# Two graph layers on one core: the order of the first loads, and which engine does the set-up of the tables and batch norms

## The chip, the core and the metric

The kernel runs on 1 core of one Trainium2 chip, in one launch, with all arithmetic in float32. The metric is the device time in microseconds (us): the median of 3 runs before the change is 1963.95 us (1963.61 to 1965.49).

The engines are called as the profile calls them: PE is TensorE (matmul), PEld its weight load, DVE is VectorE, ACT is ScalarE, POOL is GpSimd, SP is SyncE. SPq, ACTq and so on are their instruction queues, from which DMAs are issued too.

## The reference

For each of 128 batches of 128 nodes with D = 256 features, layer 0 is a residual graph convolution, and layer 1 a convolution block, a distance-weighted message pass and a GRU. Cut to what the change touches:

```python
# layer 0, per batch:  x [128, 256], adj [128, 128]
norm  = (adj.sum(-1) + 1e-6) ** -0.5
f_hom = adj @ ((x @ theta) * norm) * norm
f_het = x @ W_h
gate  = sigmoid(x @ W_t + b_t)
x     = layernorm(x + elu(gate * f_hom + (1 - gate) * f_het))
# layer 1: 1x1 convolution, batch norm 1, relu, convolution of 17 taps along the nodes, batch norm 2
h = relu(bn1(conv1d(x.T, conv1_w)))
x_conv = relu(bn2(conv1d(h, conv2_w, pad=8)) + x.T)
# ... messages A @ relu(x @ w_msg + b_msg) with A = exp(-dist), then a GRU cell, then a layernorm
```

`bn(h) = h * scale + (b - m * scale)` with `scale = g / sqrt(v + 1e-5)`: four vectors of 256 each for both norms. The kernel does the 17-tap convolution through a cosine and sine transform of length L = 136, so it needs a table of cosines and sines (`T`, and `A` for the nodes), which it computes on the chip.

## The kernel before

**Three stages.** Stage A does layer 0 and the 1x1 convolution for 64 pairs of batches (J = 2), and turns the 17-tap weights into their transform on the side. Stage B multiplies in the transformed domain. Stage C does the rest of layer 1. The change lies in the set-up and in the first rounds of stage A.

**The rounds of stage A.** `a_round(t)` runs for t = -1 to 63 under a schedule written out by hand: on each engine, instructions stand in the order of the code, and an engine's queue is strictly in order. Round t does the projections of pair t (`l0_project`: `f_ps`, `gate_ps` on PE; `hom`, `het` from ACT), in the middle of which `between()` puts the gate of pair t-1, and behind which `beside()` puts the turn of the next x (`l0_turn`, DVE transposes of `xb` to `xT`), the ELU and statistics of pair t-1 (`l0_elu`) and the degrees of the next adjacency (`l0_degrees`: two PE transposes, a DVE reduce, and `inv_sqrt`, two small POOL instructions). Then follow the layer norm of pair t-1 (`l0_norm`; its `rstd` too comes from `inv_sqrt` on POOL), the 1x1 convolution of pair t-3, the DMA issues on SP, and `l0_mix` of pair t. From pair 4 on the turn of the next x stands at the end of the round, and the next round's `f_ps` waits for it. `xT` has one buffer apart from that of pair 1, so the turn of pair 3 waits until PE has read pair 2's.

**The set-up that is woven in** is written as generators, and each `next(...)` emits one part at its place:

- `tables` (`table`, L211 on) computes the table on tiles of 128x272: range reduction on DVE, then a polynomial of degree 8 in `w` (L239 to L242), then three small instructions that make sums and differences of cosine and sine (L248 to L250). All of it is on DVE; it has one `yield`, so the first part stands in round -1 ahead of the turn of pair 0, the second behind the degrees of pair 0.
- `norms` (`batch_norms`): part 1 turns the first norm's vectors on PE (`vec_ps`, L260), copies them on DVE (`col`, L261) and takes `inv_sqrt` on POOL; part 2 is three small DVE instructions and four ACT `diag`; part 3 is a PE broadcast (`row_ps`) from which DVE makes `shift1` (L276) and scales `conv1_w` (L278). The parts stand in rounds 0, 1 and 2.
- `ways` (`way_back`): part 1 spreads a piece of `A` into `AL` on DVE (L283) and clears tiles on POOL; part 2 turns both on PE and makes `S` and `SL` on DVE (L294, L295).

**The first loads.** SP issues the four parts of the first pair's x (`xb`), then `adjT` of pair 0, then `W_t`, then x and adjacency of pair 1. ACT issues `theta`, `W_h`, `b_t`, a table load and a tanh, and eight small loads for the norms (`vec`, `col`). The part ahead of the rounds is ordered by the framework's scheduler. The compiled program gives its DMAs eight completion semaphores in turn, so that each DMA waits at its issue for the eighth before it to have landed.

## Time and profile before

| | |
|---|---|
| median of 3 runs (lowest, highest) | 1963.95 us (1963.61, 1965.49) |
| the profiled execution: device time | 1964.43 us |
| its span, from first to last instruction | 1962.6 us |
| what lies around the span | 1.8 us |
| PE, DVE, ACT, POOL busy, share of the span | 99%, 77%, 38%, 34% |
| granted PE clock, mean | 0.998 |
| first real matmuls start (adjacency of pair 0; first `f_ps`) | 8.95 us; 9.19 us |
| first `f_ps` of pairs 1, 2, 3, 4 | 16.13, 22.37, 32.41, 42.16 us |

Times in the views are from the start of the span. The timeline gives start, duration, engine, line, operation, output <- inputs, shapes, the number of merged instructions, and in brackets how long the engine had been idle before and what ended that. The chain of waits gives start, length and what the end of the kernel hung on at that moment.

### The profile page before, as it was taken

To read this page: it belongs to the slowest core of one execution; us is meant where nothing else is said; L and a number is where in the kernel's file an instruction comes from. 1 tells how busy PE (TensorE), PEld (TensorE's weight loads), DVE (VectorE), ACT (ScalarE), POOL (GpSimd) and SP (SyncE) were. 2 spreads that over 40 slices of the span, in tenths; PEclk is the share of its full clock that TensorE was granted. 3 is DMA by queue.
4 is the path that set the end of the run, shared out by engine and by line. 5 is a ranking of instruction groups with operands and counts; after the bars stand their busy time and mean duration, and the time that the engine had idled before them with its cause. 6 is when DMAs were issued, how large, how long until landed. Compare 5 with 4: busy or idle time off the path is not lost.

```text
span 1962.6 us, 26741 instructions
## 1 busy us (share of the span) xinstructions
PE 1938.2 (99%) x8539; PEld 1323.9 (67%) x8539; DVE 1502.2 (77%) x3031; ACT 738.7 (38%) x1493; POOL 670.6 (34%) x887
## 2 busy tenths in 40 slices
PE   8999999999999999999999999999999999999997
PEld 5666666666666888866666666666666666666664
DVE  8888888888888644477777777877778777787776
ACT  4666666666666311122223322222222232223222
POOL 2111111111111355544344434434433452543431
PEclk9999999999999999999999999999999999999999
DMA  6787777877776899952212212221221222121100
GB/s 175 209 239 220 232 213 232 244 226 221 224 230 188 282 324 334 321 184 93 71 59 72 82 60 65 72 71 60 82 80 45 72 82 70 61 77 38 43 28 22
DMA packets 334660, 279.90 MB, mean 143 GB/s; under 512 B 150735, under 2 KB 276921, under 8 KB 334521
## 3 DMA queue, kind: packets, MB, share of 16 engines
q1 hardware_dynamic: 327817, 272.68, 45.1%
q10 hardware_dynamic: 6704, 5.52, 0.9%
q8 instruction: 69, 1.13, 0.2%
q14 instruction: 70, 0.57, 0.1%
HBM read 173.26 MB, written 104.86 MB: 142 GB/s over the span
## 4 chain that ended last, share of the span: by engine, by line
PE 94%; DVE 3%; DMA 1%; ACT 1%; issue 1%; POOL 1%; SPq 0%; ACTq 0%; POOLq 0%; DVEq 0%
PE g_ps L1123 43%; PE f_ps L357 11%; PE y_ps L806 6%; PE gate_ps L362 5%; PE conv_ps L449 5%; PE msg_ps L977 4%; PE coef_ps L470 3%; PE z_ps L819 3%; PE conv_ps L923 3%; PE nmp_ps L1055 3%; PE mix_ps L383 3%; PE w_ps L486 2%; PE wl_ps L513 1%; PE conv_ps L930 1%; PE adj_ps L337 1%
## 5 line engine op out<-in xcount | busy, mean ns | idle before, releaser
L318 ACT ACTIVATE y<-y,nb_b,rstd_b 128x256 f32<-128x256 f32 x128 | 70.0, 593 | 562.3 <-DVE nb_b L316 562.3
L357 PE MATMUL f_ps<-w,xT 128*128 128x512 f32 x512 | 244.6, 600 | 3.0 <-DVE xT L427 1.8
L1166 POOL TENSOR_TENSOR u<-u,p 128x512 f32<-128x512 f32 x63 | 79.9, 1268 | 249.5 <-DVE p L1146 240.9
L357 PEld LDWEIGHTS f_ps<-w,xT 128*128 128x128 f32 x512 | 89.1, 189 | 103.4 <-issue 67.1
L1123 PE MATMUL g_ps<-t_h,sh 128*128 128x384 f32 x384 | 156.8, 490 | 0.0
L1123 PE MATMUL g_ps<-t_c,sc 128*128 128x384 f32 x384 | 155.2, 486 | 0.0
L1123 PE MATMUL g_ps<-t_m,sm 128*128 128x384 f32 x384 | 155.2, 486 | 0.0
L362 PEld LDWEIGHTS gate_ps<-w,xT 128*128 128x128 f32 x512 | 97.2, 190 | 68.3 <-issue 53.6
L192 POOL TENSOR_SCALAR rstd_a<-mv_a 128x2 f32<-128x2 f32 x64 | 12.2, 191 | 362.2 <-DVE mv_a L309 257.6
L362 PE MATMUL gate_ps<-w,xT 128*128 128x256 f32 x512 | 131.5, 379 | 0.1
L806 PE MATMUL y_ps<-wb,H 128*128 128x256 f32 x544 | 128.4, 379 | 0.0
L814 POOL TENSOR_TENSOR ws<-wb 128x512 f32<-128x512 f32 x67 | 93.9, 1404 | 88.3 <-PE z_ps L819 52.0
L449 PE MATMUL conv_ps<-conv_w,x1T 128*128 128x259 f32 x512 | 122.6, 381 | 1.0 <-DVE x1T L427 1.0
L366 ACT ACTIVATE hom<-f_ps,norm 128x256 f32<-128x256 f32 x128 | 60.7, 474 | 141.8 <-PE f_ps L357 133.5
L806 PEld LDWEIGHTS y_ps<-wb,H 128*128 128x128 f32 x544 | 103.4, 190 | 14.0
L1082 ACT ACTIVATE o<-o 128x1024 f32<-128x1024 f32 (+1 forms) x65 | 67.6, 1040 | 113.6 <-POOL o L1167 58.7
L449 PEld LDWEIGHTS conv_ps<-conv_w,x1T 128*128 128x128 f32 x512 | 97.1, 190 | 16.4 <-PE w_ps L486 1.8
L1123 PEld LDWEIGHTS g_ps<-t_c,sc 128*128 128x128 f32 x384 | 73.0, 190 | 50.9
L1123 PEld LDWEIGHTS g_ps<-t_m,sm 128*128 128x128 f32 x384 | 73.0, 190 | 50.9 <-DVE sm L1071 0.2
L1123 PE MATMUL g_ps<-w_hhT_w,cx1T 128*128 128x384 f32 x256 | 105.1, 492 | 0.0
L1123 PE MATMUL g_ps<-w_ihT_w,nmpT 128*128 128x384 f32 x256 | 103.8, 487 | 1.2 <-ACT nmpT L1059 1.2
L1123 PE MATMUL g_ps<-w_ihT_w,xcT 128*128 128x384 f32 x256 | 103.6, 486 | 1.2 <-ACT xcT L944 1.2
(243 smaller groups left out, 4400.9 us busy)
## 6 DMA issues: line engine op xcount, KB each, us to landing
wb<-w_d SPq DMA_DIRECT2D x68, 512.0 KB
w_d<-w_o SPq DMA_DIRECT2D x32, 1024.0 KB
y_d<-yb SPq DMA_DIRECT2D x68, 256.0 KB
x<-in_x SPq DMA_DIRECT2D x64, 256.0 KB
x_d<-x SPq DMA_DIRECT2D x64, 256.0 KB
cx1T<-x1T_d SPq DMA_DIRECT2D x64, 256.0 KB
yt<-y_d SPq DMA_DIRECT2D x32, 512.0 KB
cx<-x_d SPq DMA_DIRECT2D x32, 512.0 KB
```

The costliest lines, as they stand in the source:

```text
L318: nc.scalar.activation(dst[:, q, :], src[:, q, :], AF.Identity, bias=nb[:, q : q + 1], scale=rstd[:, q : q + 1],)
L357: nc.tensor.matmul(pf, lhsT=xT[:, c, nodes(j)], rhs=w0[:, c, 0 : 2 * D], start=(c == 0), stop=(c == NC - 1),)
L362: nc.tensor.matmul(pg[:, j * D : (j + 1) * D], lhsT=xT[:, c, nodes(j)], rhs=w0[:, c, 2 * D : 3 * D], start=(c == 0), stop=(c == NC - 1),)
L366: nc.scalar.activation(hom[:, j, :], pf[:, 0:D], AF.Copy, scale=norm[:, j : j + 1])
L383: nc.tensor.matmul(pm[:, j * D : (j + 1) * D], lhsT=adjT_[:, j, :], rhs=hom[:, j, :], start=True, stop=True,)
L449: nc.tensor.matmul(ph[:, 0 : D + CO], lhsT=s["x1T"][:, c, nodes(j)], rhs=conv1_w[:, c, :], start=(c == 0), stop=(c == NC - 1),)
L806: nc.tensor.matmul(py[:, blk, :], lhsT=coefs(blk if k == 0 else 2 * k + 1 - blk, c), rhs=w[:, blk, c, :], start=(c == 0), stop=(c == NC - 1),)
L814: nc.gpsimd.tensor_tensor(ws, w[:, 0], w[:, 1], ALU.add)
L977: nc.tensor.matmul(pm[:, pr * P : (pr + 1) * P], lhsT=s["fh"][i][:, pr, :], rhs=factors["g"][i], start=True, stop=True, skip_group_check=True,
L1082: nc.scalar.activation(rz, rz, AF.Tanh, scale=0.5)
L1123: nc.tensor.matmul(pg[:, lo : lo + 3 * P], lhsT=s[f"f{kind}"][i][:, pr, :], rhs=factors[kind][i], start=(k == 0), stop=(k == 2), skip_grou ...
L1166: nc.gpsimd.tensor_tensor(u4, u2, p5, add)
```

## The change

- `load(0)`, the adjacency of pair 0, is issued on SP ahead of the four parts of x. `W_t` goes from SP to ACT, behind `W_h`.
- `b_t` is loaded behind the loads of pair 1 in the order of the code, on ACT.
- The eight small loads for the norms leave ACT: they are issued on SP in round 0, ahead of `conv1_w`. Part 1 of `norms` goes from round 0 to the head of `beside()` in round 1; parts 2 and 3 stay.
- `table` has four `yield`s in place of one. The second half of the range reduction comes behind the turn of pair 0. The polynomial and the sums and differences go to POOL; a DVE instruction of the form (acc + c) * w becomes two there, a `tensor_scalar` and a `tensor_tensor`, so 9 DVE instructions for the polynomial become 17 on POOL (9 `tensor_scalar`, 8 `tensor_tensor`), and 3 small ones for the sums and differences become 4. They stand in three pieces: behind the degrees of pair 0 (round -1), behind those of pair 1 (round 0), and in round 1 behind part 2 of `norms`.
- `shift1`, `S` and `SL` are made by ACT in place of DVE, and `AL` by POOL in place of DVE.

```diff
     st.update((p, {}) for p in range(NP))
+    load(0)
     load_blocks(0, 1)
-    load(0)
     for j, name in enumerate(("L0_gnn_theta", "L0_gnn_W_h", "L0_gnn_W_t")):
-        (nc.sync if j == 2 else nc.scalar).dma_start(
+        nc.scalar.dma_start(
             w0[:, :, j * D : (j + 1) * D], a[name].rearrange("(p c) e -> p c e", c=NC)
         )
-    b_t = rows("L0_gnn_b_t", 0, D)
...
-    for i, q in enumerate("vmgb"):
-        nc.scalar.dma_start(vec[i * NC : (i + 1) * NC], ...)
-        nc.scalar.dma_start(col[:, i, 1, :], ...)
     load_blocks(1, 1)
     load(1)
+    b_t = rows("L0_gnn_b_t", 0, D)
+
+    def load_norms():
+        for i, q in enumerate("vmgb"):
+            nc.sync.dma_start(vec[i * NC : (i + 1) * NC], ...)
+            nc.sync.dma_start(col[:, i, 1, :], ...)
...
         v.scalar_tensor_tensor(u, r, -1.0, r, ALU.mult, ALU.max)
+        yield
         v.tensor_scalar(r, u, -1.0, float(L), ALU.mult, ALU.add)
...
         v.tensor_mul(w, r, r)
         yield
-        v.tensor_scalar(acc, w, co[8], None, ALU.mult)
-        for i in range(7, 0, -1):
-            v.scalar_tensor_tensor(acc, acc, co[i], w, ALU.add, ALU.mult)
-        v.scalar_tensor_tensor(
-            dst.rearrange("p k m -> p (k m)"), acc, 1.0, r, ALU.add, ALU.mult
-        )
+        g = nc.gpsimd
+        g.tensor_scalar(acc, w, co[8], 0.0, ALU.mult, ALU.add)
+        def step_(i):
+            g.tensor_scalar(acc, acc, co[i], 1.0, ALU.add, ALU.mult)
+            g.tensor_tensor(acc, acc, w, ALU.mult)
+        for i in range(7, 4, -1):
+            step_(i)
+        yield
+        for i in range(4, 0, -1):
+            step_(i)
+        yield
+        g.tensor_scalar(acc, acc, 1.0, 1.0, ALU.add, ALU.mult)
+        g.tensor_tensor(dst.rearrange("p k m -> p (k m)"), acc, r, ALU.mult)
...
-        v.tensor_sub(both, sin, cos)
-        v.scalar_tensor_tensor(sin, sin, -1.0, cos, ALU.mult, ALU.subtract)
-        v.tensor_copy(cos, both)
+        g.tensor_tensor(both, sin, cos, ALU.subtract)
+        g.tensor_tensor(sin, sin, cos, ALU.add)
+        g.tensor_scalar(sin, sin, -1.0, 0.0, ALU.mult, ALU.add)
+        g.tensor_copy(cos, both)
...
-        nc.vector.tensor_copy(shift1, tr[:, D : 2 * D])
+        nc.scalar.activation(shift1, tr[:, D : 2 * D], AF.Copy)
...
-        nc.vector.tensor_copy(AL, A[:, P:M].unsqueeze(1).to_broadcast([P, P // ML, ML]))
+        nc.gpsimd.tensor_copy(AL, A[:, P:M].unsqueeze(1).to_broadcast([P, P // ML, ML]))
...
-        nc.vector.tensor_scalar(S, tS[:, 0:P], back, None, ALU.mult)
-        nc.vector.tensor_scalar(SL, tS[:, P : 2 * P], 2.0 / L, None, ALU.mult)
+        nc.scalar.activation(S, tS[:, 0:P], AF.Copy, scale=back)
+        nc.scalar.activation(SL, tS[:, P : 2 * P], AF.Copy, scale=2.0 / L)
...
         def beside():
+            if t == 1:
+                next(norms)
             if 0 <= t < SOON:
                 l0_turn(t + 1)
             on(t - 1, l0_elu)
             if 0 <= t < SOON:
                 l0_degrees(t + 1)
+            if t == 0:
+                next(tables)
...
             on(t + 1, l0_turn)
+            if t == -1:
+                next(tables)
             on(t + 1, l0_degrees)
         if t == -1:
-            next(tables, None)
+            next(tables)
         if t == 0:
+            load_norms()
             nc.sync.dma_start(conv1_w[:, :, 0:D], ...)
             nc.sync.dma_start(conv1_w[:, :, D:], ...)
-            next(norms)
         if t == 1:
             next(norms)
+            next(tables, None)
             next(ways)
```

More of the change, by code (lines that the diff above doesn't have):

```diff
@@ L180, in gnn_layers_kernel @@
     col = setup.tile([P, 4, 2, NC], F32, tag="col", name="col")
-    for i, q in enumerate("vmgb"):
-        nc.scalar.dma_start(
-            vec[i * NC : (i + 1) * NC], a[f"L1_gnn_bn1_{q}"].rearrange("(c p) -> c p", p=P)
-        )
-        nc.scalar.dma_start(col[:, i, 1, :], a[f"L1_gnn_bn2_{q}"].rearrange("(p c) -> p c", c=NC))
     load_blocks(1, 1)
     load(1)
+    b_t = rows("L0_gnn_b_t", 0, D)
+    def load_norms():
+        for i, q in enumerate("vmgb"):
+            nc.sync.dma_start(
+                vec[i * NC : (i + 1) * NC], a[f"L1_gnn_bn1_{q}"].rearrange("(c p) -> c p", p=P)
+            )
+            nc.sync.dma_start(
+                col[:, i, 1, :], a[f"L1_gnn_bn2_{q}"].rearrange("(p c) -> p c", c=NC)
+            )
     def inv_sqrt(dst, src, eps, width):
@@ L237, in table @@
         yield
+        g = nc.gpsimd
         co = [(-1.0) ** i / math.factorial(2 * i + 1) for i in range(9)]
-        v.tensor_scalar(acc, w, co[8], None, ALU.mult)
-        for i in range(7, 0, -1):
-            v.scalar_tensor_tensor(acc, acc, co[i], w, ALU.add, ALU.mult)
-        v.scalar_tensor_tensor(
-            dst.rearrange("p k m -> p (k m)"), acc, 1.0, r, ALU.add, ALU.mult
-        )
+        g.tensor_scalar(acc, w, co[8], 0.0, ALU.mult, ALU.add)
[10 more added lines that the diff above has]
+        g.tensor_tensor(dst.rearrange("p k m -> p (k m)"), acc, r, ALU.mult)
         cos, sin = T[:, 2:M:2], T[:, 3:M:2]
         both = setup.tile([P, M // 2 - 1], F32, tag="both", name="both")
-        v.tensor_sub(both, sin, cos)
-        v.scalar_tensor_tensor(sin, sin, -1.0, cos, ALU.mult, ALU.subtract)
-        v.tensor_copy(cos, both)
+        g.tensor_tensor(both, sin, cos, ALU.subtract)
+        g.tensor_tensor(sin, sin, cos, ALU.add)
+        g.tensor_scalar(sin, sin, -1.0, 0.0, ALU.mult, ALU.add)
+        g.tensor_copy(cos, both)
     scale = const.tile([P, 2 * NC], F32, tag="scale", name="scale")
```

## The prediction

> **What bounds the kernel now.** I read the page first, then the busy time by stretch, then the chain of waits in order of time, then the timelines of PE and DVE, at last the durations of single lines. The page's first line of engines and of the chain:

> ```profile
> PE 1938.2 (99%) x8539; PEld 1323.9 (67%) x8539; DVE 1502.2 (77%) x3031; ACT 738.7 (38%) x1493; POOL 670.6 (34%) x887
> PE 94%; DVE 3%; DMA 1%; ACT 1%; issue 1%; POOL 1%; SPq 0%; ACTq 0%; POOLq 0%; DVEq 0%
> ```

> The end hangs on PE for 94% of the time; the rest is nearly all ahead of 42 us. Busy time by stretch (length; then PE, PEld, DVE, ACT, POOL):

> ```profile
> 0.00:9.00 9.00, 5.03 (x29) 4.87 (x30) 5.15 (x17) 1.49 (x2) 2.24 (x15) 1.00 0.53 125
> 9.00:27.70 18.70, 18.62 (x65) 11.37 (x66) 16.51 (x41) 8.08 (x20) 5.74 (x14) 1.00 0.66 170
> 27.70:42.20 14.50, 12.90 (x49) 7.26 (x47) 13.35 (x33) 8.40 (x21) 2.67 (x6) 1.00 0.72 202
> 42.20:61.70 19.50, 19.38 (x84) 12.94 (x85) 16.51 (x37) 13.12 (x31) 3.55 (x8) 1.00 0.74 217
> ```

> Three limits in a row: loads up to 9 us (PE's 5 us there are warm-up), PE from 9.0 to 27.7 (0.08 us idle), DVE from 27.7 to 42.2 (PE idle 1.6), then PE for good. So I ask one thing: when does the first `f_ps` of pair 4 start? It is 42.16 now. PE has no room to make up a delay behind it, so its shift is the kernel's shift, one to one. The chain of waits shows the hand-over:

> ```profile
> 7.20 3.90 DMA w<-in_L_gnn_W_t
> 11.15 1.13 PE gate_ps L362 x4
> ...
> 26.83 0.88 PE gate_ps L362 x4
> 27.71 0.02 issue
> 27.73 0.03 DVE xT L427
> ...
> 41.48 0.63 DVE xT L427
> 42.11 0.04 issue
> 42.16 1.98 PE f_ps L357 x4
> ```

> The total gain is capped by this: what the start gives, plus PE's 1.6 us.

> **The start.** PE's first real work waits for adjacency 0 (8.95). SP could issue that only at 6.32: it stood 3.3 us for an x part, by the eight-semaphore rule of the program. After the change the order is theta, adjacency, `W_h`, x, `W_t`, x, `b_t`, x, and the ninth, the fourth x part, waits for theta. Theta lands at 4.76 now (ACT's third small load, which waits for it, issues at 4.79); with 128 KB of adjacency ahead I take 5.0. The issue takes 0.5 and the landing 2.0 (adjacency 0: issued 6.32 to 6.67, PE starts 8.95), so x is there at 7.5; the turn takes 0.71 (L427); `f_ps` starts at 8.3, against 9.19: -0.9. Bounds: x at 6.1, when `W_h` lands now (-2.4), or at 8.0, if the 384 KB that now come ahead add 1.7 us at 230 GB/s to the 6.3 at which the third part lands now (-0.4). `W_t` lands early, which takes away the 0.2 us between `f_ps` and `gate_ps` at 11.15; `vec_ps` (0.22, pitch 0.15) leaves this stretch. Pair 1's `f_ps` is 1.2 earlier.

> **The polynomial off DVE: 0.** L239 to L250 hold DVE from 9.73 to 14.60. But PE is busy throughout, and pair 1's turn, right behind them, ends at 15.28, 0.85 ahead of the `f_ps` (16.13) that needs it. The 4.9 us only make DVE wait later; had the cover been gone, they'd be worth what exceeds 0.85.

> **The new wait: `col` behind PE.** Round 1's `beside()` now begins with the copy of `vec_ps`, which PE makes behind pair 1's `gate_ps`. In DVE's queue pair 2's turn, pair 0's ELU and statistics, and so its layer norm, stand behind it.

> ```profile
> 19.19 0.70 DVE L427 STREAM_TRANSPOSE xT<-xb 128x512 f32<-128x512 f32 x1
> 20.43 1.03 PE L362 MATMUL gate_ps<-w,xT 128*128 128x256 f32 x4
> 21.29 0.38 PE L337 MATMUL adj_ps<-ident,adjT 128*128 128x128 f32 x2
> 23.69 0.16 DVE L316 SCALAR_TENSOR_TENSOR nb_a<-mv_a,rstd_a 128x2 f32<-128x2 f32 x1 [0.19 <-POOL rstd_a L193]
> 27.73 0.71 DVE L427 STREAM_TRANSPOSE xT<-xb 128x512 f32<-128x512 f32 x1 [0.49 <-PE gate_ps L362]
> ```

> Today pair 2's turn starts at 19.19, ahead of that `gate_ps`. After: `gate_ps` gives PE free at 21.29 - 1.2 = 20.1, `vec_ps` is done at 20.3, the copy takes 0.15, the turn starts at 20.4: **+1.2**. The norms' loads don't hold this up: eight issues on SP of about 0.35 each behind adjacency 2, near 11 to 14 us, land by 16.6; were they later than 20, each us would count in full. What they push back on SP is covered by the 5.2 us SP stands still from 20.0 to 25.18.

> **The polynomial on POOL.** No row has a POOL `tensor_scalar` of this width. From below: a memset of 128x1024 takes 0.944, 0.9 ns an element, and with the 0.19 of the small L192 that makes 0.42 for 272. From above: iota's 2.2 ns an element, 0.75. I take 0.42, since a scalar instruction with one input streams like the memset. A `tensor_tensor` of 128x256 takes 0.726 alone (L1070), so 0.77 for 272; 0.85 if disturbed. Dependent ones are 0.08 apart. The first piece is 4 x 0.42 + 3 x 0.77 + 7 x 0.08 = 4.6 us, the second 4 x 1.35 = 5.4, the third about 2.9. In POOL's queue: pair 0's `norm` ends at 11.3 (turn 8.2, second half of the reduction 1.5, reduce 0.4, `inv_sqrt` 1.1), first piece to 15.9, pair 1's `norm` to 17.0 (ACT takes it at 17.0, 0.5 late, which PE does not feel), second piece to 22.4, with 0.9 of waits for DVE (below) 23.3, the batch norms' `inv_sqrt` 1.2, and only then pair 0's `rstd`: 25.5. DVE comes for it (`nb_a`) at 24.8. It stands 0.7 instead of 0.19: **+0.55**.

> **Contention.** DVE and POOL hold each other up, where DVE has two inputs from SBUF:

> ```profile
> L1070 POOL TENSOR_TENSOR sh<-cx1T x32: 719/725/736, 834.8 to 1852.4; 128x256 f32<-128x256 f32 x32
> L1070 POOL TENSOR_TENSOR sc<-xcT x32: 717/779/1192, 853.9 to 1890.5; 128x256 f32<-128x256 f32 x32
> L1070 DVE TENSOR_TENSOR sm<-nmpT x32: 417/678/951, 855.5 to 1925.8; 128x256 f32<-128x256 f32 x32
> ```

> The `sc` and `sm` runs overlap: 0.42 becomes 0.95 on DVE, 0.72 up to 1.19 on POOL. From 855.5 to 858.9 both go round in 0.87 us, less than 0.42 + 0.72, so only the streaming part excludes. At that rate the two ELU instructions wait 0.4 in sum and the tiny `scale` and `shift` ones 0.5; `AL` leaves DVE (-0.15): **+0.75**. [...]

> So DVE reaches pair 3's turn 1.2 + 0.55 + 0.75 = 2.5 later than its free time of 27.25, at 29.7; the 0.48 that it waited there for PE is used up. Shift: **+2.0**.

> **The four copies.** Behind the turn, DVE now spends 0.33 + 0.26 + 0.20 on `shift1`, `S`, `SL`. But pair 2's ELU (36.94) needs ACT's exp (36.27 to 36.90), which ends right when DVE is ready. ACT's queue between `nb_a` of pair 1 and that exp is full: two layer norms 1.0, the four `w_o` 2.0, hom and het 0.74, exp 0.63. With the three copies (0.33, 0.26, 0.26, by het's and diag's rows) this chain lengthens by 0.85, of which the 0.19 that ACT now stands idle for DVE ahead of the exp is cover. DVE's saving isn't earned: **+0.65** instead of -0.8.

> **Sum:** -1.2 at the start is inside the first term, which counts from PE; 2.0 + 0.65 = **+2.65 us**. Against the profiled execution's 1964.43 that is 1967.1; that execution lies 0.5 above the median, so I forecast 1966.6. A measurement of this kernel can tell about 0.2%, 3.9 us, from no change.

> **Rivals.** *The start wins* (0.18): x lands at 6.1, the scalars are cheap and POOL is done before DVE asks. Then the turn of pair 2 starts 1.5 sooner than above, at 18.9, `nb_a` finds its `rstd`, DVE is free for pair 3's turn at 26.8, and 14.43 - 0.8 later, at 40.4, pair 4 starts: -1.7, 1962.3. For it: SP's long gap. Against: theta's lane wait, and that PE's 0.08 us of slack up to 27.7 turns an early start into an earlier wait for DVE. *POOL becomes the bound* (0.20): at 0.75 and 0.85 the first two pieces take 3.2 us more, all of it behind `rstd`: +5.85, 1969.8. DVE already waits there, so it decides as soon as a scalar instruction takes over 0.58: 8 x 0.16 = 1.3 more makes +3.9. For it: 17 dependent instructions in a queue that the layer norm needs; against: memset's row. *Hidden* lies between: if waits and start cancel, 0, which is in the forecast's low end.

> **How the numbers follow.** Forecast 0.55, from 0 to +4.5, 0.16 of it over +3.9; the start wins 0.18, none of it beyond -3.9; POOL the bound 0.20; 0.07 for a gain over 3.9 that no case here reaches (another order of the later stages). Slower 0.36, within 0.57, faster 0.07. The range takes in most of both rivals: 1962.6 to 1969.8.

> **What would show it.** Right: first `f_ps` near 8.3; DVE idle some 2 us ahead of the `col` copy, ended by PE `vec_ps`; `nb_a` of pair 0 waiting 0.7 for POOL; pair 2's ELU waiting over 1 us for ACT's exp; pair 4's `f_ps` near 44.8. Wrong: a POOL scalar of 0.6 or more, x landed by 6.5, or a shift that appears behind 62 us.

## The result and the profile after

The change makes the kernel slower: 1971.97 us median (1969.24 to 1972.79, five runs) against 1963.95; the ratio is 1.0038, 95% interval [1.0027, 1.0049]. The forecast was 1966.6 and the range ended at 1969.8. The profiled execution is the fastest of the five, 1969.24 us with a span of 1967.5, 4.9 more than before.

The page's lines of engines and of the chain, after:

```profile
PE 1938.7 (99%) x8539; PEld 1324.0 (67%) x8539; DVE 1498.1 (76%) x3015; ACT 739.4 (38%) x1496; POOL 683.3 (35%) x909
PE 92%; DVE 3%; DMA 1%; POOL 1%; ACT 1%; issue 1%; SPq 0%; POOLq 0%; DVEq 0%; ACTq 0%
```

PE's busy time has grown by 0.5 us, so the other 4.4 of the 4.9 us are PE standing. Busy time in the same stretches as before (length; PE, PEld, DVE, ACT, POOL; then granted clock):

```profile
0.00:9.00 9.00, 5.15 (x30) 4.91 (x30) 3.41 (x13) 1.49 (x2) 2.24 (x15) 1.00 0.73 179
9.00:27.70 18.70, 18.39 (x63) 11.15 (x63) 11.71 (x30) 5.67 (x13) 14.52 (x25) 1.00 0.48 118
27.70:42.20 14.50, 11.17 (x37) 6.05 (x37) 12.61 (x26) 9.54 (x25) 5.90 (x16) 0.88 0.63 176
42.20:61.70 19.50, 18.32 (x81) 12.01 (x80) 16.86 (x39) 12.57 (x29) 3.54 (x8) 1.00 0.68 195
```

DVE has its time back up to 27.7 (11.71 instead of 16.51), POOL carries it (14.52 instead of 5.74). But from 27.7 to 42.2 PE stands for 3.3 us, and the column of the granted clock reads 0.88 where it was 1.00.

The chain of waits, start and pair 4:

```profile
0.72 3.20 DMA w<-in_L_gnn_theta
3.92 0.02 issue
3.94 4.59 DMA xb<-in_x
8.52 0.02 issue
8.55 0.71 DVE xT L440
...
44.96 0.63 DVE xT L440
45.59 0.04 issue
45.63 1.98 PE f_ps L370 x4
```

The fourth part of x waits for theta to land (3.92) and then takes 4.59 us; the first `f_ps` starts at 9.31 (before 9.19), pair 4's at 45.63 (before 42.16). What happens between, first DVE's timeline, then POOL's:

```profile
21.18 0.17 DVE L274 COPY col<-vec_ps 128x8 f32<-128x8 f32 x1 [2.21 <-PE vec_ps L273]
21.36 0.71 DVE L440 STREAM_TRANSPOSE xT<-xb 128x512 f32<-128x512 f32 x1
...
26.73 0.16 DVE L329 SCALAR_TENSOR_TENSOR nb_a<-mv_a,rstd_a 128x2 f32<-128x2 f32 x1 [0.97 <-POOL rstd_a L195]
...
28.27 1.26 DVE L410 SCALAR_TENSOR_TENSOR hom<-gate,hom 128x512 f32<-128x512 f32 x1
...
30.63 0.70 DVE L440 STREAM_TRANSPOSE xT<-xb 128x512 f32<-128x512 f32 x1
...
36.89 0.75 DVE L291 TENSOR_TENSOR conv_w<-conv_w,row_ps 128x256 f32<-128x256 f32 x2 [0.79 <-ACT shift L289]
...
40.42 0.69 DVE L419 SCALAR_TENSOR_TENSOR gate<-gate,x 128x512 f32<-128x512 f32 x1 [0.36 <-ACT gate L413]
```

```profile
12.21 0.42 POOL L243 TENSOR_SCALAR table_acc<-table_w 128x272 f32<-128x272 f32 x1
...
13.21 0.76 POOL L247 TENSOR_TENSOR table_acc<-table_acc,table_w 128x272 f32<-128x272 f32 x1
...
23.19 1.07 POOL L247 TENSOR_TENSOR table_acc<-table_acc,table_w 128x272 f32<-128x272 f32 x1
24.34 0.20 POOL L194 TENSOR_SCALAR scale<-col 128x4 f32<-128x4 f32 x1
24.63 1.01 POOL L195 TENSOR_TENSOR scale<-scale,neg_half 128x4 f32<-128x4 f32 x1
25.72 0.19 POOL L194 TENSOR_SCALAR rstd_a<-mv_a 128x2 f32<-128x2 f32 x1
25.99 0.70 POOL L195 TENSOR_TENSOR rstd_a<-rstd_a,neg_half 128x2 f32<-128x2 f32 x1
```

DVE stands 2.21 us for `vec_ps`, so pair 2's turn starts at 21.36 instead of 19.19; then 0.97 for pair 0's `rstd`, which POOL reaches at 25.72, behind the second piece of the polynomial and the batch norms' `inv_sqrt`. Pair 3's turn is at 30.63 instead of 27.73, and behind it DVE waits 0.79 and 0.36 for ACT. PE's timeline where it stands:

```profile
29.59 0.70 PE L396 MATMUL mix_ps<-hom,adjT 128*128 128x256 f32 x2 [1.82 <-ACT hom L379]
31.80 1.22 PE L396 MATMUL mix_ps<-hom,adjT 128*128 128x256 f32 x2 [1.50 <-ACT hom L379]
32.81 1.92 PE L288 MATMUL row_ps<-diag,ones 128*128 128x512 f32 x2
45.63 0.70 PE L370 MATMUL f_ps<-w,xT 128*128 128x512 f32 x1 [1.18 <-DVE xT L440]
```

ACT's first `hom` of pair 2 stands in its queue behind the layer norm and `diag` of round 1, which wait for `nb_a`; the second stands behind an exp that waits for DVE's ELU of pair 1, which is late by `nb_a` too. ACT's timeline:

```profile
26.92 1.09 ACT L331 ACTIVATE x<-hom,nb_a,rstd_a 128x256 f32<-128x256 f32 x2 [0.50 <-DVE nb_a L329]
...
28.50 0.68 ACT L285 ACTIVATE diag<-ident,shift 128x128 f32<-128x128 f32 x2
29.09 0.45 ACT L379 ACTIVATE hom<-f_ps,norm 128x256 f32<-128x256 f32 x1
...
30.75 0.63 ACT L413 ACTIVATE gate<-gate 128x512 f32<-128x512 f32 x1 [0.94 <-DVE gate L412]
31.28 0.46 ACT L379 ACTIVATE hom<-f_ps,norm 128x256 f32<-128x256 f32 x1
```

So the late `nb_a` stops PE at pair 2's mix, 14 us ahead of pair 4's `f_ps`, at which the prediction looked. Right behind it PE's own matmuls last nearly twice as long: `row_ps` takes 1.92, where the kernel before has:

```profile
28.86 1.02 PE L275 MATMUL row_ps<-diag,ones 128*128 128x512 f32 x2
```

### The profile page after: what moved, and what is told of

It reads as the page before. It is cut to its first block, busy times and chain, and to the rows that moved or that the text cites. A ratio compares the mean times of both kernels' runs of the same rounds, so it can differ in the third digit from the quotient of the medians.

```text
span 1967.5 us, 26754 instructions
## 1 busy us (share of the span) xinstructions
PE 1938.7 (99%) x8539; PEld 1324.0 (67%) x8539; DVE 1498.1 (76%) x3015; ACT 739.4 (38%) x1496; POOL 683.3 (35%) x909
## 3 DMA queue, kind: packets, MB, share of 16 engines
q1 hardware_dynamic: 328137, 272.43, 45.1%
q8 instruction: 69, 1.13, 0.2%
## 4 chain that ended last, share of the span: by engine, by line
PE 92%; DVE 3%; DMA 1%; POOL 1%; ACT 1%; issue 1%; SPq 0%; POOLq 0%; DVEq 0%; ACTq 0%
PE g_ps L1143 43%; PE f_ps L370 10%; PE y_ps L826 6%; PE conv_ps L462 5%; PE gate_ps L375 5%; PE msg_ps L997 4%; PE coef_ps L483 3%; PE z_ps L839 3%; PE conv_ps L943 3%; PE nmp_ps L1075 3%; PE mix_ps L396 2%; PE w_ps L499 2%; PE wl_ps L526 1%; PE conv_ps L950 1%; PE adj_ps L350 1%
```

## The experiments

All times stand beside runs of the kernel before on the same chip, whose medians lie between 1963.87 and 1964.54. "f_ps 4" is the start of pair 4's first `f_ps` in the run's profile (before: 42.16); the last column lists the stretches of that profile, ahead of the last microseconds, in which the granted clock was 0.5 (start, length).

| run | median us (lowest to highest) | ratio to before, 95% | f_ps 4 | at half clock, us |
|---|---|---|---|---|
| the change | 1971.97 (1969.24 to 1972.79) | 1.0038 [1.0027, 1.0049] | 45.63 | 31.7: 3.4 |
| after_again | 1971.41 (1970.12 to 1972.24) | 1.0033 [1.0021, 1.0046] | 46.63 | 9.0: 3.4; 32.9: 3.4 |
| poly_dve | 1969.11 (1967.46 to 1970.89) | 1.0026 [1.0016, 1.0035] | 45.87 | 32.0: 6.8 |
| col_late | 1970.64 (1969.16 to 1971.63) | 1.0033 [1.0021, 1.0045] | 46.61 | 8.8: 3.4; 32.7: 3.4 |
| copies_dve | 1972.70 (1970.60 to 1974.02) | 1.0043 [1.0030, 1.0055] | 49.65 | 8.9: 3.4; 32.8: 10.2 |
| pe_warm | 1969.90 (1968.52 to 1970.41) | 1.0028 [1.0017, 1.0040] | 45.21 | 45.9: 3.4 |
| warm_all | 1970.50 (1969.63 to 1971.87) | 1.0032 [1.0019, 1.0044] | 46.66 | none |
| warm_mid | 1968.90 (1967.99 to 1971.08) | 1.0026 [1.0016, 1.0037] | 46.92 | 9.2: 3.4 |
| wt_sync | 1969.07 (1968.49 to 1971.78) | 1.0025 [1.0015, 1.0035] | 44.70 | none |
| poly_dve_col_act | 1966.89 (1966.34 to 1968.74) | 1.0012 [1.0003, 1.0021] | 43.30 | none |
| loads_only | 1967.29 (1965.87 to 1969.19) | 1.0016 [1.0007, 1.0025] | 42.87 | none |
| poly_pool_only | 1968.11 (1966.02 to 1969.80) | 1.0017 [1.0008, 1.0026] | 45.16 | 8.4: 3.4; 32.3: 3.4 |
| norms_sp | 1965.04 (1963.85 to 1965.57) | 1.0001 [0.9992, 1.0010] | 41.07 | none |
| before_warm | 1969.52 (1966.24 to 1970.92) | 1.0022 [1.0013, 1.0031] | 44.62 | none |
| less_warm | 1965.65 (1964.78 to 1967.25) | 1.0009 [1.0000, 1.0018] | 42.50 | 7.7: 3.4 |
| adj_first | 1963.31 (1962.86 to 1964.01) | 0.9996 [0.9987, 1.0005] | 41.16 | none |
| adj_first_again | 1964.17 (1963.01 to 1967.52) | 1.0000 [0.9991, 1.0009] | 41.08 | none |

### The parts of the change, undone one by one

**poly_dve**: the changed kernel, polynomial and sums back on DVE in round -1.

```diff
-        g.tensor_scalar(acc, w, co[8], 0.0, ALU.mult, ALU.add)
...
+        v.tensor_scalar(acc, w, co[8], None, ALU.mult)
+        for i in range(7, 0, -1):
+            v.scalar_tensor_tensor(acc, acc, co[i], w, ALU.add, ALU.mult)
...
```

> The changed kernel with the table's polynomial and its last four operations back on VectorE, all in round -1; everything else of the change stays. Theory 'GpSimd's queue': the polynomial in GpSimd's queue and what it takes from VectorE make the layer norm of pair 0 late, TensorE then stands for the hom of pair 2 (1.82 and 1.50 us) and its clock falls. Without it nb_a of pair 0 waits 0.2 us instead of 0.97, the two ELU operations last 0.70 instead of 0.84 and 0.78, nb_a comes at 25.6 instead of 26.73, TensorE waits under 1.5 us in all for hom, the granted clock stays at 1.00 from 27 to 37 us, pair 4's f_ps starts at 43.5 to 44.3 instead of 45.63, and the time is 1967 to 1968.5. Rival 'col': the copy of vec_ps ahead of pair 2's turn sets all of it; then nb_a stays above 26.2, pair 4's f_ps above 45.0, the time at 1971 or more.

The median fell by 2.9, to 1969.11. `nb_a` waited 0.19 and PE's stand for `hom` shrank from 3.3 to 1.9 us, but `nb_a` came at 26.41: pair 1's turn now stood behind the table on DVE, PE came to it 0.65 later, and DVE again stood 1.99 us for `vec_ps`. Neither theory is right alone: POOL's wait and the one for `vec_ps` lie one behind the other, and taking one away leaves the other. The clock didn't stay at 1.00 either: this profile has two windows at half clock from 32.0.

**col_late**: the changed kernel, `next(norms)` in `beside()` behind the degrees.

```diff
-            if t == 1:
-                next(norms)
             if 0 <= t < SOON:
                 l0_turn(t + 1)
...
                 l0_degrees(t + 1)
+            if t == 1:
+                next(norms)
```

> The changed kernel with the copy of vec_ps (and its inverse square root) moved in round 1 from ahead of pair 2's turn to behind pair 2's degrees. Theory 'col': pair 2's turn starts near 19.2 instead of 21.36, and everything behind it is 2 us earlier; pair 4's f_ps at 43.0 to 43.6, the time 1967 to 1968. Theory 'GpSimd's queue': the turn is earlier, but nb_a of pair 0 then waits for GpSimd, whose second piece still ends at 24.3: with the batch norms' inverse square root no longer ahead, rstd ends near 25.2, nb_a waits 1.5 to 2 us and comes at 25.2 instead of 26.73; pair 4's f_ps at 44.0 to 44.3, the time 1968.5 to 1970.

Pair 2's turn came at 20.49 although this execution started with a half-clock stretch that cost it about 1.2 us; `nb_a` waited 0.87 and came at 25.82, as the second theory had it. Both expected a gain of 2 us or more, and it was 1.3: with the `inv_sqrt` of the norms now behind `rstd`, DVE stood 2.27 us for `scale` (28.25), and PE 1.12 and 1.94 for `hom`. The wait was moved, not removed.

**poly_dve_col_act**: poly_dve with the copy of `vec_ps` on ACT, which is idle there.

```diff
-        nc.vector.tensor_copy(col[:, :, 0, :], ...)
+        nc.scalar.activation(col[:, :, 0, :], ..., AF.Copy)
```

> poly_dve with the copy of vec_ps on ScalarE, which stands idle there, instead of VectorE; of the change there stay the loads' order and the copies. Theory: nothing then stands ahead of pair 2's turn but VectorE's own work: turn at 20.0 instead of 22.1, rstd of pair 0 finds GpSimd free, nb_a at 24.3 to 24.6 (26.41 in poly_dve, 23.69 in the kernel before), TensorE waits under 0.5 us for hom, no window at half clock at 32 us, pair 4's f_ps at 42.3 to 43.2, 1964 to 1965.5 with a spread under 2 us. Rival: the copies on ScalarE or the loads carry a share of the loss by themselves; then pair 4's f_ps stays at 44 or more.

Here the wait for `vec_ps` is gone and that for `rstd` is down to 0.40, and the time is 1966.89, 5.1 under the change. DVE's timeline, three of its lines:

```profile
24.65 0.16 DVE L321 SCALAR_TENSOR_TENSOR nb_a<-mv_a,rstd_a 128x2 f32<-128x2 f32 x1 [0.40 <-POOL rstd_a L195]
...
34.56 0.75 DVE L283 TENSOR_TENSOR conv_w<-conv_w,row_ps 128x256 f32<-128x256 f32 x2 [0.80 <-ACT shift L281]
...
38.08 0.69 DVE L411 SCALAR_TENSOR_TENSOR gate<-gate,x 128x512 f32<-128x512 f32 x1 [0.36 <-ACT gate L405]
```

The two waits for ACT (0.80 and 0.36) are there without any half clock: they belong to the copies on ACT. Pair 4 is 1.14 late; the time was 1.4 over what had been expected, of which 0.76 was lost behind pair 4.

**loads_only**: the same with `shift1`, `S`, `SL` and `AL` back on DVE.

```diff
-        nc.scalar.activation(shift1, tr[:, D : 2 * D], AF.Copy)
+        nc.vector.tensor_copy(shift1, tr[:, D : 2 * D])
-        nc.gpsimd.tensor_copy(AL, ...)
+        nc.vector.tensor_copy(AL, ...)
-        nc.scalar.activation(S, tS[:, 0:P], AF.Copy, scale=back)
-        nc.scalar.activation(SL, tS[:, P : 2 * P], AF.Copy, scale=2.0 / L)
+        nc.vector.tensor_scalar(S, tS[:, 0:P], back, None, ALU.mult)
+        nc.vector.tensor_scalar(SL, tS[:, P : 2 * P], 2.0 / L, None, ALU.mult)
```

> poly_dve_col_act with the four copies back on VectorE: of the change there stay the loads' order, W_t on ScalarE and the split of the table's first part around pair 0's turn, with the copy of vec_ps on ScalarE. Theory: the copies on ScalarE are worth +0.4 us (pair 2's ELU at 38.08, 1.14 late, where nb_a of pair 1 was 0.76 late), so pair 4's f_ps is at 42.8 to 43.0 instead of 43.30 and the time at 1966.4 to 1966.6 instead of 1966.9; the loads alone are +0.7 us. Rival: the copies are free on ScalarE; then 1966.9 or more.

Pair 4's `f_ps` at 42.87: the copies on ACT cost 0.43 (one profile each, both without half clock), and what is left of the change (the loads, the table's split first part, part 1 of `norms` behind pair 1's `gate_ps`) 0.71, which no run takes apart further. The median went the other way (+0.4); this profile loses 1.8 us between 600 and 700 us, more than any other, so the copies' price is read at pair 4 and not from the medians.

**copies_dve**: the same diff, applied to the changed kernel.

> The changed kernel with the four setup copies (shift1, S, SL, AL) back on VectorE. The prediction put them at +0.65 us on ScalarE instead of a gain of 0.8, so taking them back should give 0.65 us: pair 4's f_ps at 45.0, ELU of pair 2 no longer waiting (0.36) for the exp. Theory 'no worth': VectorE's 0.8 us of work takes the place of its waits of 0.79 and 0.36 us there, pair 4's f_ps within 0.3 of 45.63 and the time within 0.5 of the changed kernel's 1972.

Inconclusive on the copies: this profile has half clock for 3.4 us at the start and for 10.2 us from 32.8 on, and that is more than the copies can be worth. It is the pair above that sizes them.

**poly_pool_only**: the kernel before with the polynomial, the sums and `AL` on POOL, at the change's places, and nothing else.

```diff
         def beside():
...
+            if t == 0:
+                next(tables)
...
         if t == -1:
-            next(tables, None)
+            next(tables)
...
         if t == 1:
             next(norms)
+            next(tables, None)
             next(ways)
```

> The kernel before with one part of the change: the table's polynomial and its last four operations on GpSimd in the change's three pieces at the change's places, and AL, which reads the table, on GpSimd too. Loads, the copy of vec_ps and the other three copies as before. Theory: GpSimd reaches pair 0's rstd only at 24 to 25 (first piece to 15.6, pair 1's norm, second piece to 22 to 23, the batch norms' inverse square root), nb_a comes at 25.0 to 25.4 instead of 23.69 with a wait over 1 us, TensorE stands 0.5 to 1.5 us for the hom of pair 2, pair 4's f_ps is 1.3 to 2.0 us late, the time 1965.5 to 1966.5, and 1.7 more in runs in which a window falls to half clock. Rival: with pair 2's turn on time the polynomial on GpSimd is free (its cover in the change was only lost to the copy of vec_ps); then 1964 to 1964.5.

The polynomial alone is enough to lose. DVE's timeline and POOL's, which mesh:

```profile
18.24 1.10 DVE L407 SCALAR_TENSOR_TENSOR hom<-gate,hom 128x512 f32<-128x512 f32 x1
19.37 0.78 DVE L408 SCALAR_TENSOR_TENSOR het<-hom,het 128x512 f32<-128x512 f32 x1
20.19 0.87 DVE L409 TENSOR_SCALAR gate<-het 128x512 f32<-128x512 f32 x1
...
26.62 0.16 DVE L326 SCALAR_TENSOR_TENSOR nb_a<-mv_a,rstd_a 128x2 f32<-128x2 f32 x1 [0.97 <-POOL rstd_a L193]
```

```profile
18.88 0.74 POOL L243 TENSOR_SCALAR table_acc<-table_acc 128x272 f32<-128x272 f32 x1
19.70 1.07 POOL L244 TENSOR_TENSOR table_acc<-table_acc,table_w 128x272 f32<-128x272 f32 x1
```

Undisturbed, the three DVE instructions take 0.69, 0.69 and 0.43, and the two on POOL 0.42 and 0.76. The four executions at a mean clock of 0.998 take 1966.02 to 1966.74, 1.5 to 2.2 us over the median of the kernel before; the other seven, at 0.997 and less, 1967.28 to 1969.80.

### The clock

In all traces the granted clock changes only at steps of 3.413 us, on a grid that lies differently in every execution (the change: 1.00 from 4.41 to 31.72, 0.50 to 35.13, 1.00 to 1960.25; the kernel before: 1.00 from 4.50 to 1953.51). For each window of full clock I added up the time in which a matmul record runs and noted the clock of the next window. Ordered by that share, over the 18 profiles (before, after, 16 runs), around the edge:

| TensorE busy in the window | kernel, window's start | next window |
|---|---|---|
| 0.205 | the change, 28.3 | half |
| 0.246 | less_warm, 4.3 | half |
| 0.374 | after_again, 5.6 | half |
| 0.403 | col_late, 5.4 | half |
| 0.450 | pe_warm, 42.5 | half |
| 0.467 | poly_dve, 28.6 | half |
| 0.471 | pe_warm, 5.0 | full |
| 0.476 | before, 4.5 | full |
| 0.488 | after_again, 643.9 | full |
| 0.554 | the change, 4.4 | full |

From the first of these windows to 1945 us none breaks the order: all 13 under 0.468 are followed by half clock, none above is. One does at the very end, in adj_first_again: a window from 1948.8, busy for 0.42, is followed by full clock. So the edge is not sharp in this share, from which some matmul records can be missing. The kernel before escapes by 0.01, at its start; its slower executions (four of the 29 beside warm_mid, 1965.31 to 1966.08 at 0.997) fit a grid that falls worse, but none of them was profiled, and a fifth at 0.997 took 1963.39. In poly_dve two stands of 0.94 and 0.96 us were enough for half clock (the window from 28.60 is busy for 1.59 of 3.41 us), as one of 1.88 us was in pe_warm: there the sum decided and not the longest stand.

**pe_warm**: matmuls of no use in PE's stand ahead of pair 2's mix, into the unused half of its bank.

```diff
         for j in range(J):
+            if p == 2:
+                for _ in range(4 if j == 0 else 3):
+                    nc.tensor.matmul(pm[:, D : 2 * D], lhsT=adjT_[:, 0, :], rhs=w0[:, 0, 0:D],
+                                     start=True, stop=True)
             nc.tensor.matmul(pm[:, j * D : (j + 1) * D], lhsT=adjT_[:, j, :], rhs=hom[:, j, :], ...)
```

> The changed kernel with seven 128x256 matmuls of no use put in ahead of pair 2's two mix matmuls (four and three, into the unused half of the same bank), to fill the 1.8 and 1.5 us in which TensorE stands there. Theory 'clock': TensorE's stand is what lowers the granted clock from 31.5 to 35 us; filled, the clock stays at 1.00, row_ps takes 1.0 instead of 1.92 us, VectorE's conv_w no longer waits 0.79 us for ScalarE's shift, pair 4's f_ps starts near 44.8 instead of 45.63, the five times lie within 0.5 us of each other like the kernel's before (1963.5 to 1965.5) instead of over 3.5 us, and the median is 1968 to 1970. Rival: VectorE sets the time there whatever the clock; pair 4's f_ps within 0.2 of 45.63 and the times as they were.

The clock stayed at 1.00 from 9 to 45.9, and pair 4 came at 45.21. Then PE's stand there (1.88 us in one window, busy 0.45) brought the drop that the fillers had removed earlier, and it cost 1.7: the shift against before goes from 3.05 at pair 4's first `f_ps` to 4.75 at pair 5's. That the gain at pair 4 was 0.4 and not 0.8 goes against half of the expectation: pe_warm's first `f_ps` came 0.43 earlier, so nothing of it is the clock's. DVE sets pair 4, and poly_dve_col_act above has its 0.8 us wait for ACT at full clock. Nor did the spread shrink: the three executions at 0.998 take 1968.52, 1968.72 and 1970.36.

**warm_all** and **before_warm** add 18 matmuls of 128x128 at the start and five ahead of pair 3's mix (warm_all beside those of pe_warm).

```diff
+        if p == 0:
+            for _ in range(18):
+                nc.tensor.matmul(warm[:, 0:P], lhsT=ones, rhs=ones, start=True, stop=True)
         pg = bank(f"gate_ps_{p}")
...
-            if p == 2:
-                for _ in range(4 if j == 0 else 3):
+            for _ in range({(2, 0): 4, (2, 1): 3, (3, 0): 5}.get((p, j), 0)):
```

The 18 were a mistake of mine: I took 0.11 us each, they last about 0.22 at full clock (in the kernel before 15 records, two to a matmul, took 1.63 us from 4.50 to 7.91; the 15 ahead of that took 3.35, without a clock on record), so they pushed the first `f_ps` to 10.81 and 11.48.

> The changed kernel with matmuls of no use in three of TensorE's stands: 18 of 128x128 on ones between adjacency 0's transposes and the first f_ps (1.9 us), seven of 128x256 ahead of pair 2's two mix matmuls as in pe_warm, five ahead of pair 3's (1.1 us, ahead of pair 4's f_ps). Theory 'clock': the change itself shifts pair 4 by 3 us at most, and the rest of the 8 us, and the spread of the runs, is windows of 3.4 us at half clock, which follow a window of the same length in which TensorE was busy less than about 0.47 of the time; filled, there are none: mean clock 0.998 in all runs, times within 1 us of each other, median 1966.8 to 1967.5. Rival: the slow runs have another cause (a transfer, a later stage); then the median stays at 1969.5 or more with the clock at 0.998.

> The kernel before with 18 more 128x128 matmuls in the warm-up (to 8.1 us instead of 6.1) and five 128x256 ahead of pair 3's mix. In its profile no window stands at half clock, though the one from 4.5 us has TensorE busy for only 0.48 of it, close to the edge. Theory 'clock': the median stays within 0.4 of 1964.0, and the one run in sixteen that was 1.9 us longer (1965.92, clock 0.997) has no like. If the fillers cost time by themselves, it is above 1964.5.

Neither expectation holds. warm_all has all five executions at 0.998 and yet a median of 1970.50 and a spread of 2.2 us; by the letter that is its rival, though its late start alone costs 1.5 of it. So the clock is not the only thing that spreads the times. In before_warm the five executions at 0.998 take 1966.24 to 1967.80, the six at 0.997 1969.52 to 1970.92, with nothing in between. Its profile, one of the five, shows one thing well: a first `f_ps` 2.3 late is a pair 4 and an end that are 2.5 late. PE gives nothing back.

**warm_mid** is warm_all without its first three added lines.

> warm_all without the fillers at the start, which cost 1.6 us by themselves there: the changed kernel with matmuls of no use only where TensorE stands ahead of pair 2's mix (seven of 128x256, 1.5 us of 3.3) and ahead of pair 3's (five, 1.1 us). Theory 'clock': first f_ps back at 8.9 to 9.3, no window at half clock behind 27 us, pair 4's f_ps at 45.1 to 45.4 (a shift of 2.9 to 3.2), the time at 1968.0 to 1968.8 in most runs, 3.2 to 4 us under the changed kernel's 1972; what is left above the kernel before is the shift of pair 4 and 1.3 us behind it. Rival: 1970 or more, as in pe_warm and warm_all, with the clock at 0.998.

The four executions at 0.998 take 1967.99 to 1968.90, as expected, those at 0.997 and 0.996 1970.02 to 1971.08. The profiled one is of the latter: half clock from 9.2 takes its shift from 0.24 at the first `f_ps` to 1.67 at the fourth, so this window cost 1.4, with PE working without a stand.

**less_warm**: the kernel before with a shorter warm-up; nothing that the data need is touched.

```diff
-    for _ in range(WARM):
+    for _ in range(WARM - 4):
```

> The kernel before with ten instead of 14 matmuls in the warm-up, which ends at about 5.3 instead of 6.1 us. Theory 'clock': that takes the window from 4.5 us, busy for 0.48 in the kernel before, under the edge; the window behind it, with the first f_ps, is at half clock in most runs, pair 0's eight f_ps and eight gate_ps matmuls take up to twice their time, and everything behind comes 1.0 to 1.8 us later: 1965.2 to 1966.2 with a mean clock of 0.997, though not one instruction that the data need has changed. Rival: the clock doesn't follow TensorE's idleness, or the edge lies lower; then 1964.2 as before.

```profile
4.30:7.70 3.40, 0.83 (x7) 0.64 (x6) 3.04 (x8) 0.00 (x0) 0.00 (x0) 1.00 0.61 126
7.70:11.12 3.42, 2.93 (x5) 1.50 (x6) 2.10 (x6) 0.00 (x0) 0.99 (x2) 0.50 0.73 184
```

Busy for 0.83 of 3.40 us, then half clock, and 1.7 us more at the median. That the four matmuls of no use are worth 1.7 is not shown: the interval begins at 1.0000, of this profile's loss of 1.0 only 0.3 stands ahead of 800 us and 0.7 appears at 816, and the two slowest executions (1966.86 and 1967.25) are at 0.998. That a window with this little work is followed by half clock is shown, here and by the table.

**after_again**: the changed kernel unchanged, for the trace of a usual execution.

> The changed kernel once more, for a profile of one of its usual executions: the profiled one (1969.24 us, clock 0.997, one window at half clock) was the fastest of five. Theory 'clock': an execution at 1971 to 1973 has two to four windows at half clock ahead of 45 us, one of them with the first f_ps or a second and third behind the stand at pair 2's mix, where w_ps works with 17 of 128 rows; each window whose preceding one has TensorE busy under 0.47 is at half clock and no other. Rival: the slow executions lose their 2 to 3.5 us elsewhere, behind 62 us.

```profile
5.59:9.00 3.41, 1.28 (x11) 1.04 (x10) 0.49 (x1) 0.00 (x0) 0.00 (x0) 1.00 0.96 188
9.00:12.42 3.42, 3.15 (x4) 1.51 (x5) 2.54 (x7) 0.00 (x0) 1.14 (x3) 0.50 0.78 181
29.50:32.90 3.40, 0.80 (x3) 0.39 (x3) 3.25 (x5) 2.62 (x8) 3.10 (x8) 1.00 0.70 210
32.90:36.30 3.40, 3.40 (x10) 1.75 (x14) 3.05 (x10) 0.44 (x2) 1.29 (x6) 0.50 0.48 106
```

Two windows, one of them with the first `f_ps`, as expected; pair 4 comes 1.0 later than in the first profile. This execution took 1970.23; the ones at 1971 to 1973 have a mean clock of 0.995 to 0.996, and one window is 0.0009 of the mean, so they fit two to four windows. That is counted from the mean, not seen, and three digits of the mean tell no more: 1970.12 is at 0.995 too.

### The loads

**wt_sync**: warm_all with `W_t` on SP behind x, as before, and ten fillers at the start.

```diff
-        nc.scalar.dma_start(
+        (nc.sync if j == 2 else nc.scalar).dma_start(
             w0[:, :, j * D : (j + 1) * D], ...
...
-            for _ in range(18):
+            for _ in range(10):
```

> warm_all with W_t issued by SyncE behind all x parts, as in the kernel before (and ten instead of 18 fillers ahead of the first f_ps). Theory 'share of the DMA engines': x landed at 8.5 and not at 7.5 as predicted because W_t's 256 KB now run ahead of it; then x lands at 7.0 to 7.5, first f_ps at 7.8 to 8.3, and the gain ends at the copy of vec_ps: pair 2's turn about 1 us earlier, pair 4's f_ps 0.5 to 1.0 us earlier than in warm_all, 1966.3. Rival 'lane': x waits for theta's landing ahead of its fourth part whatever else runs; then x lands at 8.2 or later and nothing changes by more than 0.3 us, or W_t, needed by gate_ps 2 us behind the first f_ps, is the new wait.

```profile
2.83 4.54 DMA xb<-in_x
7.37 0.03 issue
...
7.50 0.71 DVE xT L448
```

The fourth part of x is issued at once and lands at 7.37; first `f_ps` at 8.26, pair 4 at 44.70, 0.5 ahead of pe_warm. The nine profiles of the change's loads with nothing put ahead of the first `f_ps` have it at 8.88 to 9.43, three with the loads of before (before, less_warm, poly_pool_only) at 8.64 to 9.19: the change's order gains nothing. So the prediction's 7.5 and 8.3 were the figures for the adjacency ahead of x without `W_t` on ACT. `W_t` there is a DMA more ahead of the fourth part, which therefore waits for theta's landing (3.92; SP stands 1.1 us for this load, the eighth before it, and later 1.0 and 0.7 us for `W_h` and `W_t`, each again the eighth before) and is issued at 3.94 instead of 2.83. That wait is nearly the whole difference of 1.16 us: from its issue the fourth part took 4.54 us here and 4.59 in the change, so the 256 KB less ahead of it show next to no gain. The time of x is that of the first theory, its cause the wait at the issue. The median, 1969.07, was 2.8 over what I expected; the profile loses 1.7 of it behind pair 4.

**adj_first**: the kernel before with one line moved; run twice.

```diff
+    load(0)
     load_blocks(0, 1)
-    load(0)
```

> The kernel before with one line moved: adjacency 0 ahead of the first x on SyncE. W_t stays on SyncE, where wt_sync had x at 7.45 us. x lands at 7.4 and the adjacency long before it, first f_ps at 8.2 instead of 9.19, VectorE's polynomial starts 1 us earlier, pair 1's turn too; if nothing else is late, pair 4's f_ps is at 41.1 to 41.4 and the time at 1962.9 to 1963.4, 0.8 to 1.3 under the kernel before. Rival: the loads behind (x of pairs 1 and 2, the small loads on ScalarE) take it back; then within 0.3 of 1964.2.

> adj_first once more, beside the kernel before, to narrow its interval: 1963.3 again, 0.7 to 1.2 under the kernel before, with fewer runs at a clock of 0.997 than the kernel before has (four of 29 there, one of eleven here).

Both profiles have the first `f_ps` at 8.43 and 8.35 and pair 4 1.0 and 1.1 earlier. The medians are 0.7 under and 0.3 over the kernel before, and both intervals hold 1: no version here is shown to beat it.

### Behind pair 4

**norms_sp**: the kernel before with the norms' loads and part 1 of `norms` where the change has them, `col` copied by ACT.

```diff
-    for i, q in enumerate("vmgb"):
-        nc.scalar.dma_start(vec[...], ...)
-        nc.scalar.dma_start(col[:, i, 1, :], ...)
...
         def beside():
+            if t == 1:
+                next(norms)
...
         if t == 0:
+            load_norms()
             nc.sync.dma_start(conv1_w[:, :, 0:D], ...)
             nc.sync.dma_start(conv1_w[:, :, D:], ...)
-            next(norms)
```

> The kernel before with the batch norms' eight small loads on SyncE behind pair 3's loads and the transpose of vec behind pair 1's gate_ps, as in the change, its copy on ScalarE. Theory: the loads land by 15 us, the transpose is at 21.3, ScalarE copies it at once, the inverse square root ends by 22.6, before GpSimd is asked for pair 0's rstd; pair 4's f_ps within 0.3 of 42.16. Open is what makes the versions with the change's loads lose 0.7 to 2.1 us more behind 62 us, at the hand-overs of the stages at 640, 689 and 816 us, where the versions of the kernel before lose or gain under 0.7: if it is these loads' place on SyncE, this one loses it too and takes 1964.8 to 1965.8; if not, 1964.0 within 0.3.

Pair 4 was not within 0.3 of 42.16 but 1.09 early (the adjacency, with ACT's small loads gone, was there at 7.9), and between 600 and 700 us the kernel loses 1.44. So 1965.04 lies in the range of the expectation's first branch, but by a gain that it didn't have. PE's waits there:

```profile
PE z_ps L826 <- DVE hs L823: 1.3, 1, 1.3
PE y_ps L813 <- DVE early L559: 1.0, 1, 1.0
PE x1T_ps L442 <- ACT x L323: 0.9, 1, 0.9
```

In the kernel before, `z_ps` waits 0.8 and `y_ps` not at all. Over the 18 profiles the shift against before grows in that stretch by 0.35 to 1.8 us in eleven of the twelve with the eight loads on SP (the change: 0.98; the twelfth, warm_all: -0.15), and by -0.45 to -0.01 in the five others. That it comes with these loads' place is therefore likely, but part 1 of `norms` moved in all twelve too, and no run moves one without the other; how either, at 11 to 25 us, reaches a hand-over at 640 us is open. It was not tried to keep the loads on ACT, later.

## Why the prediction was wrong

**What held.** Pair 4's `f_ps` was the place to look at, and each delay ahead of it went to the end one to one (before_warm). The POOL prices, undisturbed, were right: `tensor_scalar` 0.42, `tensor_tensor` 0.76, gaps 0.08. The rival "POOL becomes the bound" fell with them: it needed a scalar over 0.58. Contention was put at 0.90 without `AL`'s saving; the longer DVE instructions in the change add up to about 0.8 (two ELU instructions 0.24, L410 0.57). Here the size came out by luck: the 0.5 that was put on `scale` and `shift` didn't come (0.16 to 0.17 each, as before), and L410, an ELU instruction of pair 1 that the prediction hadn't named, took 0.57 more. The wait of `nb_a` was 0.97 for 0.7, and the copies cost 0.58 there (shift 2.90 at pair 3's turn, 3.48 at pair 4) for 0.65, though as a wait of 0.79 for `shift` and 0.36 for the exp. The split of the sum agrees with the runs only in part: with the polynomial back on DVE and `col` copied by ACT pair 4 is 1.14 late, 0.43 of it by the copies, and for the 0.71 that is left then the sum had no term.

**Step "the start": failed, 1.0 us.** It had x at 7.5 and the first `f_ps` at 8.3; they were 8.53 and 9.31. The ninth-DMA wait was seen, but from the start of the issue to the landing the sum counted 2.5 us (0.5 and 2.0, from a DMA with the engines nearly to itself), and it took 4.59; the 3.90 of `W_t` in the prediction's own chain of waits was the nearer row. That theta landed at 3.92 and not at 5.0 hid 1.1 us of the error. The upper bound of x, 8.0, was too low. PE ran 0.7 later into `gate_ps` of pair 1 than I had it, so `vec_ps` was done at 21.1 and not at 20.3, and **the term for `col`** was +2.17 instead of +1.2. With that alone the sum is 3.6, against 3.48 measured in the profiled execution; that the rest fits so well is partly luck, as said.

**Missing: the clock.** The prediction read the granted clock of before (1.00) and never asked what PE's new stands would do to it. It also looked for the stand at pair 3's turn, where PE had always been the one waited for; it came at pair 2's mix, through ACT's queue, 3.3 us within two windows. In the profiled execution the window behind it cost next to nothing, since DVE sets pair 4 (45.63, against 45.21 in pe_warm, whose first `f_ps` was 0.43 earlier); in the usual ones a window at the start (1.0 at pair 4 in after_again) or more than one behind the stand would have to cost the 2 to 3.5 us more that they take. From the 1968.5 or so of warm_mid at 0.998 to the change's 1972 there are about 3.4 of the 8.0 us. That all of this is the clock is argued and not shown: no execution of the change at 1971 or more was profiled, and at 0.998 pe_warm, warm_all and wt_sync spread over 1.8 to 2.2 us.

**Missing: 1.3 us behind 62 us**, which the prediction named as a sign of its being wrong: 0.23 at 81 us, 0.98 between 600 and 700. The assumption that failed is that a shift of pair 4 is the whole shift.

So the 8.0 us are about 3.5 by the predicted path (2.65 predicted), 1.3 behind it and 3.2 that are left: 2.7 between the change's median and its profiled execution, which are put down to the clock, and 0.5 because the profiled execution of the kernel before was that much over its median. The profiled execution lies within the range, the usual one does not.

## What to carry to other kernels

Where a change makes TensorE stand, price the stand twice: once by its length, once by the granted clock of the next window (half, in all 13 cases up to 1945 us here, behind 3.41 us with less than 1.6 us of work). Several small stands within one window counted together (0.94 and 0.96 us in poly_dve), and the kernel's idle start was such a stand too (0.83 us of work in 3.40, in less_warm). Two waits one behind the other on a queue hide each other: undo both together (5.1 us here, in poly_dve_col_act) before either (1.3 in col_late and 2.9 in poly_dve) is judged. Freeing a busy engine was worth nothing where its work was covered, and the work went into the queue of another: 4.9 us taken off DVE, covered, became 12.7 us on POOL (683.3 against 670.6) ahead of a 0.9 us step that everyone waits for.
